# Sizing the gathered rows of a two-layer graph kernel on the chip: one form for up to 352 rows, or two forms for up to 336 and up to 384

## The chip, the core and the metric

The kernel runs on one core of a Trainium2 chip. The metric is the device time of one execution in microseconds. Everything is float32.

## The reference

The input x holds 32 batches of 512 rows by 512 features, and adj is one 512 by 512 matrix for all batches. Two layers are applied in turn; `_L0_gnn_ref` and `_L1_gnn_ref` are written out here:

```
# layer 0
h = maximum(layernorm(x), 0)
x = x + (einsum('nm,bmd->bnd', adj, h) @ W0 + b0)
# layer 1
h = maximum(layernorm(x), 0)
q, k, v = h @ Wq + bq, h @ Wk + bk, h @ Wv + bv          # 8 heads of 64
scores = q k^T / sqrt(64) + (1 - adj) * -1e9
x = x + softmax(scores) v @ Wo + bo
```

The entries of adj are 0 or lie between 0.05 and 1, and are random. So `(1 - adj) * -1e9` separates the entries of a row by far more than the scores do, and the softmax of row n puts all its weight on the column where adj[n, :] is largest. Layer 1 then is: for each row n take row idx[n] of h, and multiply it by Wv Wo. Several rows n share one idx, so only the distinct columns among the 512 values of idx are needed. The inputs are fixed; counting the distinct columns of the row maxima of the reference's adj gives 332.

## The kernel before, in words

A prologue (`gnn_two_layers`, lines 68 to 174) loads adj, forms adj transposed (adjT), finds the largest and second largest mask value of each row, and counts the columns in use (used, many). It also bounds the size of the scores from the norms of Wq, Wk and their biases. It then decides on the chip: if the number of columns in use is at most 32 * S = 352 (line 155) and the gap between the two largest values exceeds the bound (line 162) on all 128 partitions, the number in flag is 128 and `single_path` runs (lines 176 to 178); otherwise `general_path` with the whole attention runs.

`single_path` numbers the rows so that those in use come first, and then goes through the batches. In the steady state one pass of the loop over b (line 590) consists of three products, each in Strassen-Winograd form: `product` (line 282) cuts both operands into 2 by 2 blocks and needs seven block products (pieces p1, p5, u2, c11, c22, c12, c21) where plain blocks need eight, at the price of the sums that `sum_a` and `sum_b` make on VectorE. Each piece is one call of gemm (line 285), four matmuls of 128 by 128 weights (two chunks m of output, two k of contraction) against `half` columns, all at line 288. The profile shows each float32 matmul as two records, so one piece is eight records and one product 56. The three products are:

- layer0(b): adj h times W0, 256 columns a piece, added onto x by VectorE (line 345);
- aggregate(b + 1): adj times h of the next batch, 256 columns a piece, copied out by ScalarE (line 327) or added by VectorE (line 325);
- layer1(b - 1): the rows in use of the second h, transposed (HT), times the folded weights wvo, with WIDE = 16 * S = 176 columns a piece, taken into the tile zs by `take_z`: p1, p5, u2 and c21 by ScalarE (line 338), c11, c22 and c12 by VectorE (line 335).

Between them run transfers. `put_h` (line 463) scatters h to DRAM in the numbered order by four indirect transfers from GpSimd's queue, with a small memset of gap behind each; `get_h` (line 478) reads the first 32 * S rows back; `transpose_h` (line 515) turns them into HT in blocks of 32 by 32 on VectorE; `hT_sum` makes the sums of HT. After layer1, `put_z` (line 531) transposes zs back in two pieces (rows of blocks 6 to S, then 0 to 6) and writes it to DRAM, and `finish` (line 542) gathers from there, by indirect transfers on GpSimd that add onto x.

The order of the work is written out by hand: the loop body fills 21 lists (todo), seven for each product, with `put(batch, step, function)`, and `run` (line 565) issues one list after each piece. All engines work in the order in which their instructions were issued. `zs` has one buffer. The call of layer1 at line 681 creates it, ahead of steps 14 to 20; put_z reads it at step 20 and at step 0 of the next pass. `layer0` begins with step 0, so `finish` at step 1 and the second layer norm's power on GpSimd (line 201, steps 6 and 8) come behind the gathers in GpSimd's queue.

The first pass and the last two differ: in pass b = 31 (the last batch) layer1(29) runs in steps 7 to 13 and layer1(30) in steps 14 to 20, and batch 31 itself goes through layer 1 with all 512 rows (`layer1_rows`, line 502), without zs. So layer1 is called for batches 0 to 30: 31 products, 29 of them inside the steady passes (b = 1 to 29) and two in the last one.

Of the kernel before, what the change touches and what calls it, by code (L numbers as in the profile page):

```python
# [8 lines left out]
F32 = mybir.dt.float32  # L9
# [3 lines left out]
ALU = mybir.AluOpType  # L13
# [4 lines left out]
P = 128  # L18
HD = 64
EPS = 1e-5  # L20
NEG = 1e9
S = 11


@with_exitstack
def gnn_two_layers(ctx: ExitStack, tc: tile.TileContext, x, adj, w0, b0, wq, bq, wk, bk, wv, bv, wo, bo, out):
# [15 lines left out]
    nc = tc.nc  # L42
    B, N, D = x.shape
# [5 lines left out]
    def big(name):  # L49
# [13 lines left out]
    kept = dict(xs=xs, hs=hs, adjT=adjT, yT=yT, w0_s=w0_s, sel=sel, wv_s=wv_s, wo_s=wo_s, b0_r=b0_r, used=used,  # L63
                before=before, idx=idx, ident=ident, ones=ones, mhalf=mhalf)
# [3 lines left out]
    with ExitStack() as tmp, tc.manual_schedule():  # L68
        look = tmp.enter_context(tc.tile_pool(name="look", bufs=1))
# [82 lines left out]
                    norms[2].power()  # L152
        rows = look.tile([P, 1], F32, name="rows")
        nc.vector.tensor_reduce(rows, many[:, 0, :], AX.X, ALU.add)
        nc.vector.tensor_scalar(rows, rows, float(32 * S), None, op0=ALU.is_le)


        need = look.tile([P, 1], F32, name="need")
# [15 lines left out]
            nc.vector.max_index(idx[:, c, :], top[:, c, :], mask[:, c, :])  # L174

    single = nc.values_load(flag[0:1, 0:1])
    with tc.If(single > P - 1) as cmp:
        single_path(tc, x, wv, bv, wo, bo, out, kept)
    with cmp.Else():
        general_path(tc, x, adj, wq, bq, wk, bk, wv, bv, wo, bo, out, kept)  # L180


class Norm:
# [30 lines left out]


@with_exitstack
def single_path(ctx: ExitStack, tc: tile.TileContext, x, wv, bv, wo, bo, out, kept):

# [12 lines left out]
    nc = tc.nc  # L233
    B, N, D = x.shape
    C, DC = N // P, D // P
    HALF, WIDE = N // 2, 16 * S

    xs, hs, adjT, yT, w0_s, sel, wv_s, wo_s, b0_r, used, before, idx, ident, ones, mhalf = (
        kept[k] for k in ("xs", "hs", "adjT", "yT", "w0_s", "sel", "wv_s", "wo_s", "b0_r", "used", "before", "idx",
# [9 lines left out]
    PUT, H0S, H1, HS, HC, HT, HTS, Z, ZT, ZR = {}, {}, {}, {}, {}, {}, {}, {}, {}, {}  # L249
# [7 lines left out]
    def blk(t, chunks, cols, half=HALF):  # L257
        return t[:, 2 * chunks:2 * chunks + 2, cols * half:(cols + 1) * half]
# [23 lines left out]
    def product(a, sa, bt, sb, take, half=HALF, pieces=("p1", "p5", "u2", "c11", "c22", "c12", "c21")):  # L282


        def gemm(bank, lhs, rhs, first):
            for m in range(2):
                for k in range(2):
                    nc.tensor.matmul(bank[:, m, 0:half], lhs[:, k, m * P:(m + 1) * P], rhs[:, k, :],  # L288
                                     start=(first and m == 0 and k == 0), stop=(k == 1), skip_group_check=True)

        u, v, w = None, None, None
        for piece in pieces:
            if piece == "p1":
                u = bank = ps_m.tile([P, 2, HALF], F32, name="mm")
                gemm(u, blk(a, 0, 0), blk(bt, 0, 0, half), True)
            elif piece == "p5":
                v = bank = ps_m.tile([P, 2, HALF], F32, name="mm")
                gemm(v, sa[:, 0], sb[:, 0], True)
            elif piece == "u2":
                bank = u  # L300
                gemm(u, sa[:, 1], sb[:, 1], False)
            elif piece == "c11":
                w = bank = ps_m.tile([P, 2, HALF], F32, name="mm")
                gemm(w, blk(a, 1, 0), blk(bt, 1, 0, half), True)
            elif piece == "c22":
                bank = u
                gemm(u, sa[:, 2], sb[:, 2], False)
            elif piece == "c12":
                bank = v
                gemm(v, sa[:, 3], blk(bt, 1, 1, half), False)  # L310
            else:
                bank = u
                gemm(u, blk(a, 1, 1), sb[:, 3], False)
            meanwhile = yield
            for f in meanwhile or ():
                f()
            take(piece, bank[:, :, 0:half])
# [12 lines left out]
    def take_z(t):  # L330
        def take(piece, bank):
            i, k = PLACE[piece]
            dst = blk(t, i, k, WIDE)
            if piece in ("c11", "c22", "c12"):
                nc.vector.tensor_add(dst, bank, dst)
            else:
                for m in range(2):
                    nc.scalar.activation(dst[:, m, :], bank[:, m, :], AF.Identity,  # L338
                                         bias=cvo_c[:, 2 * i + m:2 * i + m + 1])
        return take  # L340
# [137 lines left out]
    def get_h(b):  # L478
        HC[b] = work.tile([P, S, P], F32, name="hc")
        rows = HS[b].rearrange("(s j) (q f) -> q j s f", j=32, q=4)  # L480
        for q in range(4):
            load = nc.sync.dma_start(HC[b][32 * q:32 * q + 32, :, :], rows[q][:, 0:S, :])
            for stored in PUT[b]:
                tc.add_manual_dep(load.ins, stored.ins.name, mybir.DependencyInfo(
                    mybir.DependencyClass.Sync, mybir.DependencyReason.DATA), reason="all rows")
# [29 lines left out]
    def transpose_h(b, r):  # L515
        if r == 0:
            HT[b] = adjT[:, :, 0:32 * S] if b == B - 2 else work.tile([P, DC, 32 * S], F32, name="hT")
        s0, s1 = 4 * r, min(4 * r + 4, S)
        nc.vector.transpose(HT[b][:, :, 32 * s0:32 * s1].rearrange("p c (s j) -> p s c j", j=32),
# [6 lines left out]

    def layer1(b):
        ZT[b] = work.tile([P, DC, 32 * S], F32, name="zs")
        return product(wvo, wvo_t, HT[b], HTS[b], take_z(ZT[b]), WIDE)

    def put_z(b, s0, s1):
# [51 lines left out]
    with tc.manual_schedule():  # L583
# [6 lines left out]
        for b in range(B + 1):  # L590
# [83 lines left out]
            else:  # L674
                transpose_all(0)
                run(None, todo[0:7])
            run(aggregate(b + 1) if b + 1 < B else layer1(b - 2) if b < B else None, todo[7:14])
            if b == 0:
                run(fold_weights(), todo[14:21])
            else:  # L680
                run(layer1(b - 1) if b < B and b != B - 2 else None, todo[14:21])
# [265 lines left out]
```

## Time and profile before

| what | value |
|---|---|
| time, median of three runs | 1108.0 us (1107.43 to 1109.12) |
| profiled execution | 1104.05 us, of which 1101.6 us from the first to the last instruction |
| TensorE clock granted | 0.998 |
| records of line 288 with 176 columns | 1736 |
| mean length of such a record, as listed | 313 ns |
| mean length of a record with 256 columns, as listed | 380 ns |

The page lists the busy time of each engine, the chain of work that ended last, and groups of equal instructions with count and mean length. A matmul's listed length runs from its start to its modelled end; matmuls overlap, so what a stream of them costs is read from the distance between their starts, in the timeline. PE is the matmul itself, PEld the loading of its weights, DVE VectorE, ACT ScalarE, POOL GpSimd and SP the engine whose queue starts most plain transfers.

### The profile page before, as it was taken

How to read it: one execution, taken by the hardware profiler on the slowest of the kernel's cores; microseconds unless marked ns; L12 is line 12 of the kernel's file. 1: busy time of each engine (PE TensorE's matmuls, PEld its weight loads, DVE VectorE, ACT ScalarE, POOL GpSimd, SP SyncE). 2: the span in 40 equal slices, each digit the busy share in tenths (PEclk: the TensorE clock that was granted, in tenths of full speed). 3: DMA queues.
4: the chain of work that ended last, by engine and by line, in shares of the span. 5: the costliest groups of instructions: out<-in, count | busy, mean ns of one | idle time of the engine just before them, and what ended most of it. 6: DMA issues, size and time to landing. Idle time of an engine off the chain costs nothing.

```text
span 1101.6 us, 15852 instructions
## 1 busy us (share of the span) xinstructions
PE 1079.9 (98%) x5404; PEld 953.2 (87%) x5404; DVE 907.3 (82%) x1853; ACT 358.6 (33%) x655; POOL 443.8 (40%) x491
## 2 busy tenths in 40 slices
PE   7999999999999999999999999999999999999996
PEld 3569989999989989988999998999999899999883
DVE  6869888888888888878888888888888878888863
ACT  3223323233323333322323332323332232333221
POOL 2124544333554343454333454433355434345413
PEclk9999999999999999999999999999999999999999
DMA  6362676667777667767666776666776766676537
GB/s 238 125 141 74 172 191 148 160 175 197 182 181 158 149 171 193 187 171 169 157 156 189 193 189 177 146 160 173 196 179 181 164 149 171 184 193 155 141 105 245
DMA packets 162412, 186.90 MB, mean 170 GB/s; under 512 B 14993, under 2 KB 102289, under 8 KB 162321
## 3 DMA queue, kind: packets, MB, share of 16 engines
q1 hardware_dynamic: 130672, 112.70, 37.3%
q0 software_dynamic: 27968, 66.61, 27.0%
q10 hardware_dynamic: 3680, 6.49, 1.7%
q8 instruction: 44, 0.72, 0.3%
q14 instruction: 48, 0.39, 0.2%
HBM read 96.28 MB, written 89.46 MB: 169 GB/s over the span
## 4 chain that ended last, share of the span: by engine, by line
PE 94%; DMA 1%; DVE 1%; ACT 1%; POOL 1%; issue 1%; ACTq 0%; SPq 0%; POOLq 0%; DVEq 0%
PE mm L288 89%; PE mm L139 1%; PE mm L458 1%; PE mm L372 1%; PE mm L508 1%; POOL x L544 1%; DMA x<-in_x_dram 1%; DMA yT<-z,place 1%; ACT h L212 0%; DMA z<-zr 0%; DVE x L345 0%; DVE st L194 0%; ACT zs L338 0%; POOL yT L553 0%; DVE zr L535 0%
## 5 line engine op out<-in xcount | busy, mean ns | idle before, releaser
L544 POOL DMA_INDIRECT x<-z,place x116 | 182.8, 1576 | 370.6 <-DMA z<-zr 318.7
L327 ACT COPY yT<-mm 128x512 f32<-128x512 f32 x124 | 71.8, 579 | 562.0 <-PE mm L288 527.9
L345 DVE TENSOR_TENSOR x<-mm,x 128x512 f32<-128x512 f32 x217 | 149.7, 690 | 86.2 <-PE mm L288 86.2
L212 ACT ACTIVATE h<-x,off,rstd 128x512 f32<-128x512 f32 x256 | 194.9, 808 | 36.2 <-DVE off L204 34.2
L201 POOL TENSOR_TENSOR rstd<-ve,mhalf 128x2 f32<-128x2 f32 (+1 forms) x97 | 106.0, 1093 | 222.1 <-DVE ve L200 222.1
L194 DVE BATCH_NORM_STATS2 st<-x 128x6 f32<-128x512 f32 x256 | 171.5, 670 | 9.2 <-DMA x<-in_x_dram 8.0
L288 PE MATMUL mm<-w_t,sel 128*128 128x256 f32 x744 | 171.1, 380 | 0.8 <-DVE x L345 0.8
L288 PE MATMUL mm<-adjT_s,h0s 128*128 128x256 f32 x744 | 170.8, 380 | 1.0 <-ACT yT L327 1.0
L288 PEld LDWEIGHTS mm<-w_t,sel 128*128 128x128 f32 x744 | 141.5, 191 | 20.4 <-DVE x L345 1.6
L288 PEld LDWEIGHTS mm<-adjT_s,h0s 128*128 128x128 f32 x744 | 141.6, 191 | 20.2 <-ACT yT L327 1.4
L470 POOL DMA_INDIRECT hs<-h,dest x124 | 133.7, 1078 | 30.8 <-issue 22.2
L338 ACT ACTIVATE zs<-mm,cvo_c 128x176 f32<-128x176 f32 x248 | 87.2, 403 | 98.2 <-PE mm L288 98.2
L288 PE MATMUL mm<-hTs,wvo_t 128*128 128x176 f32 x720 | 117.5, 313 | 0.6 <-ACT zs L338 0.6
L288 PE MATMUL mm<-adjT,h 128*128 128x256 f32 x496 | 117.2, 380 | 0.0
L288 PE MATMUL mm<-w_s,yT 128*128 128x256 f32 x496 | 117.2, 380 | 0.0
L288 PEld LDWEIGHTS mm<-hTs,wvo_t 128*128 128x128 f32 x720 | 109.8, 191 | 1.1 <-ACT zs L338 1.1
L288 PEld LDWEIGHTS mm<-adjT,h 128*128 128x128 f32 x496 | 94.5, 191 | 13.0 <-issue 0.5
L288 PEld LDWEIGHTS mm<-w_s,yT 128*128 128x128 f32 x496 | 93.3, 191 | 11.5 <-issue 0.5
L436 DVE TENSOR_TENSOR x<-x,b_r 128x512 f32<-128x512 f32 x128 | 86.6, 678 | 0.0
L288 PE MATMUL mm<-hT,wvo 128*128 128x176 f32 x480 | 81.4, 313 | 0.0
L288 PEld LDWEIGHTS mm<-hT,wvo 128*128 128x128 f32 x480 | 75.3, 190 | 1.5
L325 DVE TENSOR_TENSOR yT<-mm,yT 128x512 f32<-128x512 f32 x93 | 63.9, 687 | 5.8 <-PE mm L288 3.0
(146 smaller groups left out, 1278.9 us busy)
## 6 DMA issues: line engine op xcount, KB each, us to landing
out_dram<-x SPq DMA_DIRECT2D x124, 256.0 KB, 4.1
x<-in_x_dram SPq DMA_DIRECT2D x120, 256.0 KB, 5.5
hc<-hs SPq DMA_DIRECT2D x124, 176.0 KB, 3.8
z<-zr SPq DMA_DIRECT2D x120, 96.0 KB, 2.0
z<-zr SPq DMA_DIRECT2D x120, 80.0 KB, 1.9
hs<-h,dest POOLq DMA_INDIRECT x124, 5.9
x<-z,place POOLq DMA_INDIRECT x116, 5.8
x<-in_x_dram ACTq DMA_DIRECT2D x4, 256.0 KB, 5.3
```

What stands on the lines that cost most here:

```text
L139: nc.tensor.matmul(ps, hs[0][:, m, d * P:(d + 1) * P], adjT[:, m, :], start=(m == 0), stop=(m == C - 1))
L194: self.nc.vector.bn_stats(st, self.src[:, self.chunks[i], :])
L201: self.nc.gpsimd.tensor_tensor(self.rstd, ve, self.mhalf[:, 0:n], ALU.pow)
L212: self.nc.scalar.activation(dst, src, AF.Relu, bias=self.off[:, i:i + 1], scale=self.rstd[:, i:i + 1])
L288: nc.tensor.matmul(bank[:, m, 0:half], lhs[:, k, m * P:(m + 1) * P], rhs[:, k, :], start=(first and m == 0 and k == 0), stop=(k == 1), ski ...
L325: nc.vector.tensor_add(dst, bank, dst)
L327: nc.scalar.copy(dst, bank)
L338: nc.scalar.activation(dst[:, m, :], bank[:, m, :], AF.Identity, bias=cvo_c[:, 2 * i + m:2 * i + m + 1])
L345: nc.vector.tensor_add(dst, bank, dst)
L436: nc.vector.tensor_add(X[b][:, c, :], X[b][:, c, :], b0_r)
L470: stored = nc.gpsimd.indirect_dma_start(out=HS[b], out_offset=bass.IndirectOffsetOnAxis(ap=dest[:, i:i + 1], axis=0), in_=H1[b][:, i, :], ...
L544: nc.gpsimd.indirect_dma_start(out=X[b][:, c, :], out_offset=None, in_=Z[b], in_offset=bass.IndirectOffsetOnAxis(ap=place[:, c:c + 1], axi ...
```

## The change

The size of the gathered branch becomes an argument, room. Two forms of `single_path` are built, for 336 and for 384 rows in use, and the prologue chooses between them: rows becomes 2 where at most 336 columns are in use, 1 where at most 384, and 0 otherwise, so that flag holds 256, 128 or 0 (times the other test). In the form for 336 the pieces of layer1 have 168 columns in place of 176. What is moved stays at S = 11 blocks of 32 rows, that is 352: get_h, transpose_h, put_z and the buffers are as before. The columns 336 to 351 of zs, which no piece writes any more, are set to zero by a memset on GpSimd for every batch, ahead of step 14. The form for 384 has S = 12 and 192 columns. It serves inputs with more rows in use than the kernel before took into the gathered branch.

```diff
-S = 11
+ROOM = 336, 384
...
-        nc.vector.tensor_scalar(rows, rows, float(32 * S), None, op0=ALU.is_le)
+        fits = look.tile([P, 1], F32, name="fits")
+        nc.vector.tensor_scalar(fits, rows, float(ROOM[0]), None, op0=ALU.is_le)
+        nc.vector.tensor_scalar(rows, rows, float(ROOM[1]), fits, op0=ALU.is_le, op1=ALU.add)
...
     single = nc.values_load(flag[0:1, 0:1])
-    with tc.If(single > P - 1) as cmp:
-        single_path(tc, x, wv, bv, wo, bo, out, kept)
+    with tc.If(single > 2 * P - 1) as cmp:
+        single_path(tc, x, wv, bv, wo, bo, out, kept, ROOM[0])
     with cmp.Else():
-        general_path(tc, x, adj, wq, bq, wk, bk, wv, bv, wo, bo, out, kept)
+        with tc.If(single > P - 1) as cmp2:
+            single_path(tc, x, wv, bv, wo, bo, out, kept, ROOM[1])
+        with cmp2.Else():
+            general_path(tc, x, adj, wq, bq, wk, bk, wv, bv, wo, bo, out, kept)
...
-def single_path(ctx: ExitStack, tc: tile.TileContext, x, wv, bv, wo, bo, out, kept):
+def single_path(ctx: ExitStack, tc: tile.TileContext, x, wv, bv, wo, bo, out, kept, room):
...
-    HALF, WIDE = N // 2, 16 * S
+    HALF, WIDE = N // 2, room // 2
+    S = (room + 31) // 32
...
     def layer1(b):
         ZT[b] = work.tile([P, DC, 32 * S], F32, name="zs")
+        if room < 32 * S:
+            nc.gpsimd.memset(ZT[b][:, :, room:32 * S], 0.0)
         return product(wvo, wvo_t, HT[b], HTS[b], take_z(ZT[b]), WIDE)
```

## The prediction

> **What bounds the kernel now.** I read the busy times first.
>
> ```profile
> PE 1079.9 (98%) x5404; PEld 953.2 (87%) x5404; DVE 907.3 (82%) x1853; ACT 358.6 (33%) x655; POOL 443.8 (40%) x491
> ```
>
> Matmuls fill 98% of the span. Listed lengths overlap, so this alone does not prove a bound; the chain of waits does:
>
> ```profile
> PE 94%; DMA 1%; DVE 1%; ACT 1%; POOL 1%; issue 1%; ACTq 0%; SPq 0%; POOLq 0%; DVEq 0%
> ```
>
> Line 288, all pieces of the three products, carries 89.0% of that chain. So the span is a sum of matmul starts, and I want the distance between starts by width. The timeline of TensorE over one aggregate (256 columns) and the layer1 behind it (176 columns) has start, length to the end of the last, and count:
>
> ```profile
> 314.55 1.89 PE L288 MATMUL mm<-adjT,h 128*128 128x256 f32 x8
> 316.28 3.62 PE L288 MATMUL mm<-adjT_s,h0s 128*128 128x256 f32 x16
> ...
> 326.64 1.36 PE L288 MATMUL mm<-hT,wvo 128*128 128x176 f32 x8
> 327.83 2.55 PE L288 MATMUL mm<-hTs,wvo_t 128*128 128x176 f32 x16
> 330.22 1.36 PE L288 MATMUL mm<-hT,wvo 128*128 128x176 f32 x8
> 331.41 1.36 PE L288 MATMUL mm<-hTs,wvo_t 128*128 128x176 f32 x8
> 332.61 1.36 PE L288 MATMUL mm<-hT,wvo_t 128*128 128x176 f32 x8
> 333.80 1.36 PE L288 MATMUL mm<-hTs,wvo 128*128 128x176 f32 x8
> 334.99 1.24 PE L288 MATMUL mm<-w_s,yT 128*128 128x256 f32 x5
> ```
>
> Aggregate takes 326.64 - 314.55 = 12.09 us for 56 records, 215.9 ns each; layer1 takes 334.99 - 326.64 = 8.35 us for 56, 149.1 ns each. No idle time stands before any row. Last, the busy time by product, for layer0, aggregate and layer1 of that pass (width of the stretch, then PE, PEld, DVE, ACT, POOL busy):
>
> ```profile
> 302.47:314.55 12.08, 12.08 (x58) 10.67 (x57) 9.25 (x15) 0.70 (x2) 4.69 (x3) 1.00 0.54 101
> 314.55:326.64 12.09, 12.09 (x57) 10.68 (x56) 10.83 (x28) 4.59 (x7) 7.89 (x12) 1.00 0.91 239
> 326.64:334.99 8.35, 8.35 (x57) 8.35 (x56) 7.60 (x16) 5.63 (x11) 1.40 (x1) 1.00 0.73 201
> ```
>
> VectorE is the next engine: 77%, 90% and 91% of the three stretches. The clock is full.
>
> **What the Trainium skill says.** "TensorE: Matmul & The Clock Gate", section "Back-to-back issue gap", gives N / 2.4 + 2.5 ns for a record of N columns, that is linear with a small constant. Here the slope is (215.9 - 149.1) / 80 = 0.835 ns a column, twice the page's and near its N / 1.2 for a cold clock although the granted clock is 0.998; for these float32 records the measurement decides. The constant agrees: 149.1 - 176 * 0.835 = 2.1 ns. The same page, section "LDWEIGHTS (loading the stationary operand)", puts a load of 128 columns at P / 1.2, 107 ns. In the trace the eight one-column matmuls of line 147 (chain of waits, 23.45 to 24.23) show a bare load: after the first, seven loads span 0.86 us with 0.19 us for the last one's own length, so (0.86 - 0.19) / 6 = 112 ns apart. It agrees, and lies below 149. "SBUF — State Buffer", section "Who interferes with whom", says that a VectorE instruction with two SBUF inputs contends with a GpSimd instruction that reads SBUF, "not with one that only writes it"; the new memset only writes. No run here shows that yet.
>
> **Which form runs.** The count of rows in use from the reference's inputs is 332, at most 336, so flag is 256 and the form with 168 columns runs. The trace agrees as far as it can: the gathered branch ran, so the count is at most 352.
>
> **The change part by part.** *Narrower pieces.* By the line above a record of 168 columns takes 2.1 + 168 * 0.835 = 142.4 ns, well over the 112 ns of a bare load, so 6.7 ns less than 149.1. A product has 56 records: 0.374 us. The widest form checks the line: 2.1 + 512 * 0.835 = 429.6 ns, while the 32 records of line 458 take 13.97 us, 437 ns with the start of the stage in it. Of the 31 products 29 lie in steady passes where TensorE is the chain: 29 * 0.374 = 10.85 us. The last two lie in the final pass, where TensorE also waits for ScalarE's takes:
>
> ```profile
> 1063.13 1.46 PE L288 MATMUL mm<-hTs,wvo_t 128*128 128x176 f32 x8 [0.59 <-ACT zs L338]
> ...
> 1070.17 1.46 PE L288 MATMUL mm<-adjT_s,wvo_t 128*128 128x176 f32 x8 [0.80 <-ACT zs L338]
> ```
>
> There a shorter piece partly lengthens a wait; of 2 * 0.374 = 0.75 us I count half, 0.37 (bounds 0 and 0.75). Sum 11.22 us.
>
> *Shorter takes and sums.* Elements per partition fall from 352 to 336. VectorE's 512-element adds take 685 ns and its 352-element ones 516, 1.06 ns an element, so 17 ns each: three takes in the layer1 stretch, four sums in aggregate, 0.12 us a pass. ScalarE's eight takes (403 ns, 176 elements) save under 10 ns each. All lie beside matmuls and count as nothing; they only give VectorE room.
>
> *The memset*, 64 elements a partition, 31 times, is on no path. Its price lies between these two rows:
>
> ```profile
> L473 POOL MEMSET gap<- 128x1 f32 x124 | 14.4, 116 | 0.2
> L77 POOL MEMSET ones<- 128x128 f32 x1 | 0.2, 203 | 0.0
> ```
>
> that is 116 to 203 ns; I take 160. In GpSimd's order it comes behind put_h (in the first steady pass behind four look-ups as well) and ahead of the layer norm's power (line 201, four columns). In 29 of the 29 steady passes the last of put_h's four scatters ends 0.6 to 2.3 us before layer1's first matmul, and that power starts 2.1 to 3.4 us after it, having waited some 3 us for VectorE (3.03 and 3.22 in the two passes that I looked at). So the memset falls into idle time. What it waits for, put_z's last reads of zs, was over a whole product earlier. What waits for it: ScalarE's takes gain no wait in the order of instructions, and VectorE's put_z reads the columns some 7 us later. Only the last one, for batch 30, gives a VectorE transpose a new wait on GpSimd: that memset stands behind the four get_all gathers, the last of which ends at 1073.1, and the transpose starts at 1075.88. So 2.6 us of room.
>
> *Choosing.* One more 128x1 VectorE operation on the way to flag; its neighbour at line 155 takes 154 ns. TensorE waits there for VectorE (0.8 us before line 164), so I charge all of it, 0.15 us (bounds 0 and 0.2). The nested If is not reached by the first form, so the compare-and-branch of "Advanced Engine Details and Errata", section "Control Flow Timing" (108 ns), is not paid a second time; no row of the trace shows it. The transfers stay at 352 rows.
>
> Total: -10.85 - 0.37 + 0.15 = -11.1 us, 1108.0 - 11.1 = 1096.9; I say 1097.0.
>
> **The rivals.** *A, as worked out: 1097.0.* *B, another engine takes some of it.* layer1's stretch becomes 8.35 - 0.37 = 7.98 us, with 7.60 - 0.05 = 7.55 us of VectorE in it, 95%. VectorE waits for TensorE inside it only once, 0.54 us before the c11 take, and its last takes keep exactly a piece's pace. If it falls behind and the next product waits 0.2 us in each pass, 29 * 0.2 = 5.8 come back: 1102.7. Against: the layer0 behind it is 77% loaded, takes only free PSUM banks, and the last sum of yT is made 2.2 us before layer0 starts. *C, slower: the gathers come late.* GpSimd's gathers stand ahead of the power in its queue. Once in the trace they came late (first gather 17.7 us after layer1's start, mostly 15.1 to 15.5):
>
> ```profile
> 482.94 0.16 DVE L204 SCALAR_TENSOR_TENSOR off<-mv,rstd 128x2 f32<-128x2 f32 x1 [2.20 <-POOL rstd L201]
> 483.18 0.81 ACT L212 ACTIVATE h<-x,off,rstd 128x512 f32<-128x512 f32 x1 [3.04 <-DVE off L204]
> ...
> 485.70 2.00 PE L288 MATMUL mm<-adjT_s,h0s 128*128 128x256 f32 x8 [1.01 <-ACT yT L327]
> ```
>
> TensorE lost 1.2 us. get_h's read (step 16) and put_z's write now lie some 0.2 us nearer, so z could land later. If every pass fell over: 29 * 1.2 = 35 less 11.1, 1132. Against: the chain from layer1's end through put_z, gather and power is not shortened, and usual passes have over 1 us in hand. *D, nothing gained,* 1108.1: the width rounds up to 176, or the loads (191 ns listed, 152 apart) set the pace. Against: 112 ns at line 147. *E, more:* the idle of those late passes (about 2 us outside both ends) disappears: 1095.
>
> **How the numbers follow.** A 0.80, B 0.09, E 0.05, D 0.03, C 0.03. A spreads about 1.5 us to each side: three runs before spread 1.7 us, and one late pass costs 1.2. The range 1094.8 to 1100.0 takes A and E and the better half of B. Faster by over 0.2% (below 1105.8): A, B and E, 0.94; the same 0.03 (D); slower 0.03 (C).
>
> **What would show it.** Right: 168-column records 142 to 143 ns apart, layer1 7.98 us long, passes of 32.15 in place of 32.52 us, the other two products unchanged, the memset near 160 ns with no one waiting for it. B shows as waits of TensorE on VectorE behind layer1; C as gathers over 16.5 us after layer1's start and ScalarE waiting for line 204's successor; D as 149 ns. Wrong altogether would be 192 columns in the rows of line 288's successor: the other form, 56 * 31 * 16 * 0.835 ns = 23 us more.

## The result and the profile after

The changed kernel takes 1096.04 us (median of four runs, 1095.16 to 1098.71) against 1108.44 us before (1107.43 to 1109.12): ratio 0.9893, 95% interval 0.9873 to 0.9913, that is 9.6 to 14.1 us less, and 12.4 by the medians. Forecast were 1097.0 us, 11.1 less, and a range of 1094.8 to 1100.0.

The profile after is that of the slowest of the four runs, 1098.71 us. Its busy times, to be read beside those of before:

```profile
PE 1071.3 (98%) x5404; PEld 941.6 (86%) x5404; DVE 903.2 (82%) x1854; ACT 357.0 (33%) x655; POOL 445.7 (41%) x522
```

TensorE is still busy for 98%, with the same number of records; GpSimd has 31 instructions more, the memsets, and VectorE one, the second test. The timeline of TensorE over one layer1 and its neighbours is taken from the changed kernel's third profile (e10 below, which has no stop of the kind told next), with start, length to the end of the last, and count:

```profile
324.68 1.30 PE L294 MATMUL mm<-hT,wvo 128*128 128x168 f32 x8
325.82 2.44 PE L294 MATMUL mm<-hTs,wvo_t 128*128 128x168 f32 x16
328.10 1.30 PE L294 MATMUL mm<-hT,wvo 128*128 128x168 f32 x8
329.24 1.30 PE L294 MATMUL mm<-hTs,wvo_t 128*128 128x168 f32 x8
330.38 1.30 PE L294 MATMUL mm<-hT,wvo_t 128*128 128x168 f32 x8
331.52 1.30 PE L294 MATMUL mm<-hTs,wvo 128*128 128x168 f32 x8
332.66 1.89 PE L294 MATMUL mm<-w_s,yT 128*128 128x256 f32 x8
```

layer1 takes 332.66 - 324.68 = 7.98 us, 142.5 ns a record. It was 8.35 us and 149.1 ns. In the profile after, 26 of the 29 layer1 products of the steady passes take 7.97 to 7.99 us (the others 12.59, 8.23 and 8.01), and the undisturbed pass, from one layer1 to the next, 32.15 us, where it was 32.53.

The same profile shows a thing that the profile of before had not shown. In the list of ScalarE's work at the first layer1, the bracket is the idle time and what ended it; "remote" is a release that the trace cannot place:

```profile
99.58 0.59 ACT L333 COPY yT<-mm 128x512 f32<-128x512 f32 x1 [4.90 <-PE mm L294]
103.74 1.28 ACT L344 ACTIVATE zs<-mm,cvo_c 128x168 f32<-128x168 f32 x4 [3.58 <-remote]
```

ScalarE stood still for 3.6 us, TensorE for 2.7 us behind it, and from 106 to 109 us the granted clock of TensorE was 0.56. Busy times by stretch (width, then PE, PEld, DVE, ACT and POOL busy, then granted clock, DMA share and GB/s):

```profile
103.00:106.00 3.00, 1.51 (x8) 1.51 (x9) 2.14 (x5) 1.28 (x4) 1.17 (x1) 0.87 0.36 62
106.00:109.00 3.00, 3.00 (x14) 3.00 (x14) 0.22 (x1) 2.52 (x5) 0.00 (x0) 0.56 0.00 0
109.00:112.00 3.00, 3.00 (x23) 3.00 (x23) 2.86 (x6) 0.98 (x2) 0.00 (x0) 1.00 0.00 0
```

So layer1 of batch 0, the first one of the kernel, took 12.59 us there in place of 8.64, and the span of this profile is only 1101.6 - 1097.0 = 4.6 us shorter than that of before, against 12 us in the times. Whether this stop belongs to the change was the first question for the experiments.

### The profile page after: what moved, and what is told of

Read it like the earlier page. It is cut to its first block, busy times and chain, and to the rows that moved or that the text cites. A ratio compares the mean times of both kernels' runs of the same rounds, so it can differ in the third digit from the quotient of the medians.

```text
span 1097.0 us, 15882 instructions
## 1 busy us (share of the span) xinstructions
PE 1071.3 (98%) x5404; PEld 941.6 (86%) x5404; DVE 903.2 (82%) x1854; ACT 357.0 (33%) x655; POOL 445.7 (41%) x522
## 4 chain that ended last, share of the span: by engine, by line
PE 91%; DVE 3%; DMA 2%; POOL 1%; issue 1%; ACT 1%; another core or an unknown queue 0%; SPq 0%; ACTq 0%; POOLq 0%; DVEq 0%
PE mm L294 85%; PE mm L139 2%; PE mm L464 1%; PE mm L378 1%; POOL x L552 1%; PE mm L514 1%; DMA yT<-z,place 1%; DMA x<-in_x_dram 1%; DMA z<-zr 0%; DVE st L199 0%; ACT h L217 0%; DVE zr L543 0%; DVE x L351 0%; DMA hc<-hs 0%
## 5 line engine op out<-in xcount | busy, mean ns | idle before, releaser
L294 PEld LDWEIGHTS mm<-adjT_s,h0s 128*128 128x128 f32 x744 | 141.1, 190 | 20.7 <-ACT yT L333 1.6
L294 PE MATMUL mm<-hTs,wvo_t 128*128 128x168 f32 x720 | 113.7, 307 | 3.5 <-ACT zs L344 3.5
L344 ACT ACTIVATE zs<-mm,cvo_c 128x168 f32<-128x168 f32 x248 | 85.6, 397 | 88.6 <-PE mm L294 84.9
L294 PEld LDWEIGHTS mm<-hTs,wvo_t 128*128 128x128 f32 x720 | 106.0, 191 | 4.2 <-ACT zs L344 4.2
L294 PE MATMUL mm<-hT,wvo 128*128 128x168 f32 x480 | 79.4, 309 | 0.0
```

## The experiments

They ran in three sets, on three chips; the kernel before took 1104.41 us (17 runs) in the first set, 1108.06 (7) in the second and 1103.72 (17) in the third. So kernels of different sets are compared by their ratios to before. Every diff is against the changed kernel.

**Set 1: which part makes the gain.** The changed kernel again (e1), the choosing alone (e2), the narrower pieces alone (e3), and two columns less (e4).

```diff
-ROOM = 336, 384
+ROOM = 352, 384
```

for e2, and for e4

```diff
-ROOM = 336, 384
+ROOM = 332, 384
```

and for e3

```diff
-        fits = look.tile([P, 1], F32, name="fits")
-        nc.vector.tensor_scalar(fits, rows, float(ROOM[0]), None, op0=ALU.is_le)
-        nc.vector.tensor_scalar(rows, rows, float(ROOM[1]), fits, op0=ALU.is_le, op1=ALU.add)
+        nc.vector.tensor_scalar(rows, rows, float(ROOM[0]), None, op0=ALU.is_le)
...
-    with tc.If(single > 2 * P - 1) as cmp:
+    with tc.If(single > P - 1) as cmp:
...
-        with tc.If(single > P - 1) as cmp2:
-            single_path(tc, x, wv, bv, wo, bo, out, kept, ROOM[1])
-        with cmp2.Else():
-            general_path(tc, x, adj, wq, bq, wk, bk, wv, bv, wo, bo, out, kept)
+        general_path(tc, x, adj, wq, bq, wk, bk, wv, bv, wo, bo, out, kept)
```

> The changed kernel once more. If the stop of 3.6 us on ScalarE ahead of the first layer1 take (at 100 us of the profile) belongs to the program, it stands at the same place again; if it was a matter of that one execution, it is gone, the span is near 1093 us, and layer1 of batch 0 takes about 8.3 us instead of 12.59. Time 1096 us in either case.

> Two forms, for 352 and 384 rows, so that layer1 keeps 176 columns and no memset is made: the choosing alone. Theory (the columns make the gain, choosing costs 0.15 us on the way to the flag): 1108.6 us, layer1 8.35 us, the first matmul of layer0_rows 0.15 us later. Rival (a larger program with two gathered forms costs time of its own, or gains some): off by 1 us or more from 1108.4.

> One form for 336 rows with 168 columns and the memset, no second gathered form and no second test: the columns alone. Theory: 1096.0 us, the same as the changed kernel within 0.5 us. Rival (the layout of the program makes part of the gain, which the changed kernel has and this one not): 1097.5 us or more.

> Forms for 332 and 384 rows: 166 columns, the fewest that hold the 332 rows in use; memset of 20 columns. Theory (0.835 ns a column and record): 2 * 0.835 * 56 * 31 = 2.9 us less than the changed kernel, 1093.1 us; layer1 7.89 us. Rival (widths are rounded up to a multiple of 8 or 16, which 168 and 176 can't tell from a line): layer1 7.98 us and 1096 us.

| kernel | time, us | ratio to before, 95% interval | layer1 | undisturbed pass |
|---|---|---|---|---|
| e1, the changed kernel | 1092.78 | 0.9897 (0.9883 to 0.9911) | 7.98 | 32.15 |
| e2, 176 columns, two forms | 1104.08 | 0.9996 (0.9988 to 1.0005) | 8.35 | 32.53 |
| e3, 168 columns, one form | 1093.04 | 0.9897 (0.9881 to 0.9912) | 7.98 | 32.15 |
| e4, 166 columns, two forms | 1089.50 | 0.9869 (0.9854 to 0.9884) | 7.90 | 32.08 |

By the times, the columns make the gain: e3 has it all, and e2 none of it that its interval (1.3 us less to 0.6 more) would show. e4 shows that the line goes on for two columns more, with 1.12 to 1.13 us from piece to piece where 168 columns take 1.14:

```profile
323.17 1.29 PE L294 MATMUL mm<-hT,wvo 128*128 128x166 f32 x8
324.30 2.42 PE L294 MATMUL mm<-hTs,wvo_t 128*128 128x166 f32 x16
...
331.07 1.89 PE L294 MATMUL mm<-w_s,yT 128*128 128x256 f32 x8
```

331.07 - 323.17 = 7.90 us, where 7.89 was expected; nothing is rounded up to 8 or 16 columns. e4 beats both kernels on these inputs: 3.3 us less than e1 by the medians, 2.9 expected. It keeps the larger form for more rows, so only the threshold is tighter.

In e1 the stop of ScalarE was gone: layer1 of batch 0 took 8.50 us, and the span 1092.0 us. (The 1096 us expected for it missed that the kernel before, too, is 4 us faster on this chip.) Nor is it in e2, e3 and e4.

**Set 2: where the line ends, and the memset multiplied.** e5 makes the memset eight times; e6 lets the second form run; e7 and e8 narrow the pieces to 152 and 120 columns, so that they leave out layer 1 for rows that are in use.

For e5 (and later e11; 24 in e12)

```diff
-            nc.gpsimd.memset(ZT[b][:, :, room:32 * S], 0.0)
+            for _ in range(8):
+                nc.gpsimd.memset(ZT[b][:, :, room:32 * S], 0.0)
```

for e6

```diff
-ROOM = 336, 384
+ROOM = 320, 384
```

and for e7 (120 in e8)

```diff
-    HALF, WIDE = N // 2, room // 2
+    HALF, WIDE = N // 2, 152 if room == ROOM[0] else room // 2
...
-        if room < 32 * S:
-            nc.gpsimd.memset(ZT[b][:, :, room:32 * S], 0.0)
+        if 2 * WIDE < 32 * S:
+            nc.gpsimd.memset(ZT[b][:, :, 2 * WIDE:32 * S], 0.0)
```

> The memset of zs eight times in a row for every batch. Theory (it falls into time in which GpSimd waits for VectorE): seven more of 0.165 us, 1.16 us a batch, all hidden, 1096.0 us; layer1 7.98 us. Rival (GpSimd's queue is on a path, so that even one memset costs): 29 * 1.16 = 34 us more if it were wholly on the path.

> Forms for 320 and 384 rows, so that the second form runs for these inputs: 192 columns, 12 blocks moved, no memset. Theory (the same line upwards): 24 columns more than the changed kernel, 24 * 0.835 * 56 * 31 = 34.8 us, 1130.8 us; layer1 9.1 us. If the twelfth block's transposes and transfers also lie on a path, more than that.

> Pieces of 152 columns, with all else at 352 rows. It leaves out layer 1 for the rows numbered 304 to 331, whose columns of zs are set to zero, so its time is that of a smaller layer1. Theory (a line as long as TensorE is the bound): 16 * 0.835 * 56 * 31 = 23.2 us less than the changed kernel, 1073 us; layer1 7.23 us. Rival (VectorE, which has 7.5 us of work issued in layer1's stretch, sets its length): layer1 still near 7.5 us, or the products behind it wait, 1081 us or more.

> Pieces of 120 columns. It leaves out layer 1 for the rows numbered 240 to 331. By the line alone a record would take 102 ns, layer1 5.73 us, and the kernel 69.6 us less than the changed one, 1026 us. Rival 1 (a bare load of weights, 112 ns, is the floor): layer1 6.27 us, 1043 us. Rival 2 (VectorE's 7.2 us in the stretch): layer1 near 7.2 us or the same wait behind it, about 1072 us.

| kernel | time, us | ratio to before, 95% interval | layer1 | undisturbed pass |
|---|---|---|---|---|
| e5, eight memsets | 1098.81 | 0.9915 (0.9897 to 0.9933) | 7.98 | 32.15 |
| e6, second form, 192 columns | 1137.18 | 1.0256 (1.0236 to 1.0275) | 9.10 | 33.28 |
| e7, 152 columns | 1076.64 | 0.9715 (0.9695 to 0.9736) | 7.28 | 31.46 |
| e8, 120 columns | 1062.86 | 0.9587 (0.9564 to 0.9609) | 6.78 | 30.97 |

One of the four executions of e8 took 2175.65 us, for a reason that the record does not show; the ratio is that of the other three, 1062.19 to 1062.92.

Upwards the line holds: from e1 to e6, 24 columns, the pass grows by 33.28 - 32.15 = 1.13 us, and 24 * 56 * 0.835 ns is 1.12; the twelfth block adds nothing to the pass. But e6 is 28.4 us over before (26.2 to 30.5), where 16 columns over 31 products give 23.2. The rest lies at the start. From the matmul of the choice to the first one of the branch, e6 has:

```profile
27.84 0.19 PE L166 MATMUL few<-ones,sure 128*1 128x1 f32 x2
32.70 16.77 PE L464 MATMUL mm<-w_s,yT 128*128 128x512 f32 x32 [4.68 <-DVE idx L176]
```

and the first form in e10:

```profile
28.58 0.19 PE L166 MATMUL few<-ones,sure 128*1 128x1 f32 x2
30.05 13.97 PE L464 MATMUL mm<-w_s,yT 128*128 128x512 f32 x32 [1.29 <-ACT h L217]
```

4.86 us in place of 1.47 from the one to the other, and 16.77 in place of 13.97 for the 32 records, which in e6 run at a granted clock of 0.50 from 32 to 38 us. (e5, e7 and e8, on the chip of e6, have 1.48 to 1.49 us and 13.97 there, as e10 has.) That is 6.2 us. It fits: 23.2 + 6.2 = 29.4, inside the interval. In e6 the engines go to a form that lies behind another in the program. Between 27 and 33 us the trace has seven transfers of instructions (queues q8 and q14) in e6 and one in e10, and in e6 SyncE, TensorE and GpSimd all begin the branch late, between 32.00 and 32.77 us (29.59 to 30.05 in e10). So it looks as if the engines wait for their instructions; no run tried it.

Downwards the line bends. At 152 columns five of the seven pieces are still on it, 1.03 us for eight records or 129 ns, as 2.1 + 152 * 0.835 gives; layer1 is 0.06 us longer than the line. At 120 columns it is 6.78 us, where the line says 5.73. The timeline of TensorE in e8:

```profile
320.25 1.05 PE L294 MATMUL mm<-hT,wvo 128*128 128x120 f32 x8
321.13 2.08 PE L294 MATMUL mm<-hTs,wvo_t 128*128 128x120 f32 x16
323.04 1.06 PE L294 MATMUL mm<-hT,wvo 128*128 128x120 f32 x8
323.94 1.12 PE L294 MATMUL mm<-hTs,wvo_t 128*128 128x120 f32 x8
324.90 1.06 PE L294 MATMUL mm<-hT,wvo_t 128*128 128x120 f32 x8
326.04 1.15 PE L294 MATMUL mm<-hTs,wvo 128*128 128x120 f32 x8
327.03 1.90 PE L294 MATMUL mm<-w_s,yT 128*128 128x256 f32 x8
```

The shortest distance is 0.88 us for eight records, 110 ns each, not 102. That is the distance of bare loads of weights: 112 ns at line 147, and 107 by the Trainium skill, "TensorE: Matmul & The Clock Gate", section "LDWEIGHTS (loading the stationary operand)", for 128 columns. So the load is taken for the floor; a narrower piece, which would show it, was not run. The other pieces take longer than that, and the waits of e8 name one cause (us in total, times, longest):

```profile
PEld mm L294 <- DVE zs L341: 8.4, 28, 0.5
```

TensorE waits 0.3 us for VectorE's takes in 28 passes. So both rivals came in at 120 columns, the load as a floor and VectorE as a wait on top of it. Neither alone gives the 6.78 us: seven pieces at the floor are 6.2 to 6.3 us, with the wait 6.5 to 6.6, and the last 0.2 to 0.3 us stay unexplained.

All four profiles of this set show the stop of ScalarE, ending at 103.3 to 103.9 us (at 109.0 in e6, which started its batches 5.4 us later), and the profile after, on a chip where before took 1108.44 us, shows it too. So I ran the kernel before for its own profile in the last set.

**Set 3: the stop, and the memset beside the changed kernel.** e9 is the kernel before, e10 the changed kernel, e11 eight memsets, e12 twenty-four.

> The kernel before, for its own profile on the chip on which the three kernels beside it run. Theory (the stop of ScalarE ahead of the first layer1 take goes with the chip, not with the change): where the changed kernel shows it on this chip, so does this one, layer1 of batch 0 near 12.9 us in place of 8.64, and where not, not. Rival (it goes with the change, by the memset or the layout of the program): 8.64 us here whatever the changed kernel shows.

> The changed kernel on the chip of the kernel before and of the two memset kernels beside it: 11.6 us under the kernel before, as it was beside the one-form kernel.

> Eight memsets again, now beside the changed kernel on one chip. In its first profile they took 1.62 us together and GpSimd still waited 1.70 us for VectorE behind them. Theory: the same time as the changed kernel within 1 us. Rival (they cost, as the 9.3 us under the kernel before against 11.6 for the changed kernel may be read): 2 us more or above.

> Twenty-four memsets: 4.85 us by the length of eight, over the 3.2 us that GpSimd waits in the changed kernel. Theory (the idle time hides the memset and ends there): the power of the layer norm comes 1.5 us late, VectorE stands 0.7 us for it ahead of line 209 in every pass, and with 0.3 us to spare TensorE loses about 0.4 us a pass: 12 us more than the changed kernel (5 to 25). Rival (nothing of GpSimd's queue here reaches TensorE): no difference.

| kernel | time, us | ratio to before, 95% interval | layer1 of batch 0 | layer1 | undisturbed pass |
|---|---|---|---|---|---|
| e9, before | 1103.84 | 1.0002 (0.9992 to 1.0011) | 8.64 | 8.35 | 32.53 |
| e10, changed | 1091.93 | 0.9889 (0.9874 to 0.9904) | 8.49 | 7.98 | 32.15 |
| e11, eight memsets | 1094.15 | 0.9915 (0.9900 to 0.9930) | 9.53 | 7.98 | 32.15 |
| e12, twenty-four | 1112.17 | 1.0074 (1.0057 to 1.0090) | 11.93 | 8.27 | 32.44 |

No profile of this set has the stop, so e9 could not answer its question. What stands: the stop is there in all five profiles taken beside a kernel before of 1108 us (the one after and the four of set 2, all of them the changed kernel and its variants), and in none of the eight of the other two sets (seven of the changed kernel and its variants, e2 among them, and e9) or in the first profile of before, which took 1104.05 us. The changed kernel is 3 to 4 us faster on the chips without it (1092 to 1093 against 1096), and so is the kernel before (1104 against 1108); the ratios agree, 0.9893, 0.9897 and 0.9889. That speaks for a stop that both have and that goes with the chip. The kernel before has no profile from such a chip, so this and the stop's cause stay open.

Eight memsets leave the undisturbed pass at 32.15 us; in the first pass, from layer1 of batch 0 to that of batch 1, layer1 is 1.04 us longer than in e10. There the layer norm's power comes late, VectorE's take behind it too, and TensorE waits 1.28 us where it waits 0.24 in e10 (shown below):

```profile
105.60 0.16 DVE L209 SCALAR_TENSOR_TENSOR off<-mv,rstd 128x4 f32<-128x4 f32 x1 [0.94 <-POOL rstd L206]
...
107.25 1.41 PE L294 MATMUL mm<-hTs,wvo 128*128 128x168 f32 x8 [1.28 <-DVE zs L341]
```

The whole kernel is 2.2 us longer than e10 by the medians, in intervals that touch, so by the medians the expectation of the same time within 1 us was missed, as in e5, which has the same ratio. The rest of the 2.2 is within the scatter of the late passes told below. Twenty-four reach the limit in every pass. From GpSimd's, VectorE's and TensorE's lines of one pass:

```profile
330.07 5.00 POOL L537 MEMSET zs<- 128x64 f32 x24
...
335.03 1.58 POOL L206 TENSOR_TENSOR rstd<-ve,mhalf 128x4 f32<-128x4 f32 x1
...
336.64 0.16 DVE L209 SCALAR_TENSOR_TENSOR off<-mv,rstd 128x4 f32<-128x4 f32 x1 [0.93 <-POOL rstd L206]
...
338.30 1.15 PEld L294 LDWEIGHTS mm<-hTs,wvo 128*128 128x128 f32 x8 [0.27 <-DVE zs L341]
```

The power starts some 1.6 us later than its input from VectorE would let it, VectorE stands 0.93 us in front of line 209, its take of zs comes late, and TensorE waits 0.27 us for it: 32.44 - 32.15 = 0.29 us a pass, 0.4 expected. In the first pass TensorE waits 3.69 us in the same way. e12 is 20.2 us over e10, within the 5 to 25 of the expectation, but not by the steady passes alone, which give 9.5. The first pass gives 5.1 and the end 5.9, where VectorE's transpose of zs waits once for the memsets, on the wait that the prediction had named for batch 30 (us in total, times, longest):

```profile
DVE hc L544 <- POOL zs L537: 3.1, 1, 3.1
```

VectorE's adds of two inputs that ran beside the memsets of the pass shown (lines 269 to 273, 442) took 0.66 to 0.69 us, as in e10. The Trainium skill, "SBUF — State Buffer", section "Who interferes with whom", says that a GpSimd instruction that only writes does not contend with such adds; that holds here.

## Why the prediction was right

**Narrower pieces: right to the hundredth.** Forecast 142 to 143 ns, 7.98 us and passes of 32.15 us, the other products unchanged; measured 142.5 ns, 7.98, 32.15, and 12.08 to 12.09 us for the products with 256 columns. The check at 512 columns is closer than the prediction had it: from start to start the 32 records take 43.44 - 29.63 = 13.81 us, 431.6 ns each against 429.6, while the 437 has the end of the last one in it. e3, e4 and e6 show the gain going with the columns. The line rests on the trace alone: the formula that the prediction set beside it from the Trainium skill, "TensorE: Matmul & The Clock Gate", section "Back-to-back issue gap", is there the gap of an isolated matmul, with half the slope measured here, so that the two constants agree (2.1 and 2.5 ns) is no support for it.

**Twenty-nine products at 0.374 us: 28 of them.** The first steady pass gained less: layer1 of batch 0 went from 8.64 to 8.49 us (e9 to e10), 0.15 us. VectorE is late there, and its takes set the pace; TensorE waits for the last of them in e10:

```profile
106.34 1.41 PE L294 MATMUL mm<-hTs,wvo 128*128 128x168 f32 x8 [0.24 <-DVE zs L341]
```

**The last two products: I counted half of their gain, and it can't be told.** TensorE's waits for ScalarE's takes grew as feared, from 0.58 and 0.80 us in e9 to:

```profile
1052.72 1.41 PE L294 MATMUL mm<-hTs,wvo_t 128*128 128x168 f32 x8 [0.78 <-ACT zs L344]
...
1059.60 1.41 PE L294 MATMUL mm<-adjT_s,wvo_t 128*128 128x168 f32 x8 [0.91 <-ACT zs L344]
```

From the start of the first of the two products to batch 31's first matmul the time fell from 1077.00 - 1056.83 = 20.17 us to 1066.83 - 1047.22 = 19.61. But the end of the kernel came no sooner: the span ends 43.27 us after that start in e9 and 43.28 in e10. In the other profiles this stretch scatters more than the term is worth: 43.99 us in the first one of before, 44.96 and 44.38 in the one after and in e1.

**The memset: the length right, the hiding too general.** It takes 143 to 177 ns, 167 in the middle, where I took 160. In steady passes nobody waits for it and GpSimd still waits 3.16 us for VectorE behind it. In the first pass, where I had named the four look-ups ahead of it, there was little room: GpSimd waited 0.39 us in e9 and 0.20 in e10. One memset fits; eight do not (1.04 us).

**Choosing: 0.15 us charged, nothing measured.** I read the wait of 0.8 us ahead of the choice's matmul as one for VectorE. VectorE's lines and TensorE's in e9 and then in e10:

```profile
25.85 1.96 PE L139 MATMUL mm<-adjT,h 128*128 128x512 f32 x4
26.93 0.16 DVE L163 TENSOR_TENSOR sure<-sure,rows 128x1 f32<-128x1 f32 x1
27.74 0.19 PE L164 MATMUL few<-ones,sure 128*1 128x1 f32 x2
```

```profile
26.68 1.96 PE L139 MATMUL mm<-adjT,h 128*128 128x512 f32 x4
27.95 0.16 DVE L165 TENSOR_TENSOR sure<-sure,rows 128x1 f32<-128x1 f32 x1
28.58 0.19 PE L166 MATMUL few<-ones,sure 128*1 128x1 f32 x2
```

sure ends 0.65 us ahead of the matmul before and 0.47 after, and the matmul comes 1.89 and 1.90 us behind TensorE's own group of line 139. VectorE had long been done, and the matmul follows TensorE's own stream; the profile names the last release that it knows. The extra operation costs 0.2 us of VectorE and nothing of the path. So the 0.15 us came of a misread wait; it is too small for the times to show.

**The sum.** By the profiles e9 and e10, in order of time: the start 98.25 to 99.09, +0.84 us; the first pass 32.81 to 32.67, -0.14; the 27 passes behind it -9.93 (27 * 0.374 is 10.1, with some 0.2 us more of late passes against it); the pass with the change of order 45.67 to 45.29, -0.38; the end +0.01. That is 1090.5 - 1100.1 = -9.6 us. These are two single executions. The first layer1 begins at 98.25 and 98.67 us in two profiles of before, and at 98.33, 99.09 and 99.38 in three of the changed kernel, so a few tenths at the start may belong to the change or not. Over all executions the medians of the span fell by 11.1 us (1101.3 to 1090.2) in set 3 and by 11.0 in set 1. That is the forecast, and it is partly luck that it fits to the tenth, with a gain at the end that cannot be told and a charge for the choosing that was nothing.

The time outside of the first to the last instruction, the difference between time and span, fell by another 0.7 us (2.44 us in e9, 1.73 in e10, medians), which I had not forecast. It goes with the second form more than with the columns: 1.77 us in e2, which has two forms but the old columns, and 2.06 in e3, which has the new columns and one form. Its cause was not looked for. In e2 the span is 0.3 us longer than that of before, within its scatter, which hides half of it. So the times fell by 11.8 us in set 3 (10.6 to 13.9 by e10's ratio), of which the forecast accounts for 11.1.

**The rivals.** B was wrong here, though close: VectorE is busy for 7.51 us of the 7.98 in e10 (7.55 forecast), and at 152 columns TensorE lost only 0.06 us; at 120 VectorE's wait is there. Neither C nor E came: the late passes stay, for the most part at the same places. In the profile after, the one at 482 us lost 0.87 us at the same place as before:

```profile
483.39 0.16 DVE L209 SCALAR_TENSOR_TENSOR off<-mv,rstd 128x2 f32<-128x2 f32 x1 [1.90 <-POOL rstd L206]
...
486.16 1.99 PE L294 MATMUL mm<-adjT_s,h0s 128*128 128x256 f32 x8 [0.71 <-ACT yT L333]
```

Over the 27 passes the late ones lose 2.2 and 1.9 us in two profiles of before, and 2.5, 3.2 and 2.0 in three of the changed kernel: if z comes later for the change, it costs half a microsecond in all. D fell with the 142.5 ns, and e4 leaves no rounding at 168 either.

## What to carry to other kernels

Where one engine's stream is the chain, fit a line through two widths that the profile has and read the gain from it: here two numbers of one timeline gave 7.98 us for the stretch before it was run. Then ask how far the line goes: look at what else is issued in the shortened stretch (VectorE here) and at what a record costs with next to no columns (the load here). A wait that the profile puts down to an engine is checked by when that engine's instruction ended; where it ended half a microsecond before, an extra operation of 0.2 us cost nothing.

## What the runs showed of the hardware that I had not expected

- Float32 matmul records were narrowed by 8 and by 2 columns without rounding: 149.1 ns apart at 176 columns, 142.5 at 168, 141.1 at 166 (7.90 us by 56). At 120 columns the shortest distance was 110 ns, not the 102 of the line.
- Entering a branch that lies behind another one took 3.4 us longer until TensorE's first matmul, and the 32 records behind it 2.8 us longer, with a granted clock of 0.50 from 32 to 38 us (e6).
- A stop of ScalarE at one place of the program is in every profile taken beside a kernel before of 1108 us and in none of the others. In the profile after, the first layer1 took 12.59 us with it, where e1 has 8.50, and the granted clock was 0.56 for 3 us behind it.
